# Layer 3 of a four-layer block: gate chain read by ScalarE, another lead-in, half of the partition copies issued on ScalarE's DMA queue

## The chip, the cores and the metric

The kernel runs on one core of a Trainium2 chip. The metric is the device time of one execution in microseconds (us). Before the change three runs gave 3566.73, 3568.6 and 3573.8 us; the median is 3568.6 us.

## The reference, cut to what matters

The input x has 4 samples of 256 channels on a 48 by 48 grid, in float32. Four layers follow each other, each of the form x + f(gn(x)), where gn is a group normalisation with 32 groups of 8 channels. Layers 0 to 2 are an attention with 8 heads, a gated depthwise filter, and an attention with one head that ends in a batch normalisation over all samples. Layer 3 is the one that the change is about:

```python
def _L3_conv_ref(x, attn_w1, attn_w2, refine_w, refine_b):
    p = jnp.mean(xw, axis=(2, 3))
    h = jax.nn.leaky_relu(p @ attn_w1.T, SLOPE)
    a = jax.nn.sigmoid(h @ attn_w2.T)
    y = xw * a[:, :, None, None]
    y = jax.lax.conv_general_dilated(y, refine_w, window_strides=(1, 1), padding='SAME', feature_group_count=C, ...)
    y = y + refine_b[None, :, None, None]
    mu = jnp.mean(y, axis=(2, 3), keepdims=True)
    var = jnp.mean(jnp.square(y - mu), axis=(2, 3), keepdims=True)
    y = (y - mu) * jax.lax.rsqrt(var + EPS)
    return jax.nn.leaky_relu(y, SLOPE)
...
x = x + _L2_conv_ref(_gn(x), ...)
x = x + _L3_conv_ref(_gn(x), ...)
```

So layer 3 is a 3 by 3 depthwise convolution of the normalised input, times a gate per channel and sample, then an instance normalisation, a leaky relu and the residual.

## The kernel before, in words

Channels lie on the 128 partitions, in two halves k = 0, 1. Layers 0 to 2 run first, with TensorE busy almost without a break in the attention of layer 2. The end of layer 2 and layer 3 are written out as one order per engine: within a `manual_schedule` scope every engine executes its instructions in the order in which the code emits them, and waits for others through semaphores.

**Layer 2's end.** The last attention unit is folded and divided (`fold`, `divide`, L389 to L395) on VectorE, `note` (L406 to L412) takes two sums of its denominators, `w_stats` (L1084) multiplies the last third of y by the output weights and takes `bn_stats`, and L1410 to L1433 turn these into the batch normalisation's scale `sc2` and offset `bi2` and into the means of the new x.

**Layer 3's tiles.** There are 8 tiles i, one for each sample and channel half (`TILES`). A tile's input is made by `w_product` (TensorE: output weights times y) and `grow` (VectorE, L1463: scale, add x, write into the padded image `pads`), with `border` (GpSimd) around it. The convolution is done on TensorE as 32 by 32 blocks: `shifted` holds, for each group of 32 channels j, copies of its padded image on the partitions of three of four groups q (`SHIFT`), and `products` (L1604) runs 12 matrix multiplications of this on 384 columns. The copies are made by `place` and `spread_out` (L1496 to L1511): for each half h of the rows, eight copies between different partition groups by DMA on SyncE's queue (SP), and four within a group, by GpSimd for h = 0 and on SP's DMA queue for h = 1. Each is 32 partitions by 1298 elements, 162.2 KB. Three `shifted` buffers take turns.

**Slots.** A tile i has six slots from t = 6 i, one for each sixth of its columns. `events` (L1747) holds for each slot a list of (rank, function), and the functions of a slot are emitted by rank: FRONT, CONV, PRODUCT, GROW, EVICT, SMALL, MOMENTS, SQUARE, SCALE, LAST, PLACE, STORE. For tile i, counted from its t:

- slots 0 to 5: `products` (CONV); slots 2, 4, 6: `evict` (ScalarE, L1616, two slots' PSUM to SBUF with a sum); slots 3, 5, 7: `square` of the result (ScalarE, L1627); slot 3: `centre` (VectorE)
- slot 8: `moments`, `scales` (VectorE, eight small instructions and GpSimd's power), `shift` under LAST
- slots 9, 10, 11: `scale` (ScalarE, L1681); slots 10, 11, 12: `leak` and `gain` (VectorE, L1687 and L1692, under LAST); slots 11, 12, 13: `store`
- slots -9, -8, -7: `w_product` and `grow` for the tile's three thirds; slots -8, -7, -6: squares of its input (ScalarE, L1487); slots -6 and -3: `spread_out` for h = 0, 1

The gate of a sample needs its group variance and two tiny layers. `Chain` (L1513) does this once per sample, so in even tiles: `total` (VectorE) and `groups` (TensorE) in slot 1, `inverse` (VectorE reads PSUM, GpSimd's power) in slot 2, `pooled` (VectorE) and `first_layer` (TensorE) in slot 3, `hidden` (VectorE reads PSUM) and `second_layer` (TensorE) in slot 4, `gate` (ScalarE reads PSUM) and `scaled` (VectorE) in slot 5. The chain's results in PSUM lie in unused columns of the convolution's own PSUM tile (`cv`), which holds two slots; three such tiles take turns. Its first member of a slot is emitted at FRONT, its second at SMALL:

```python
def put_chain(t, parts):
    for dt, (head, tail) in enumerate(parts):
        at(t + dt, FRONT, lambda fn=head: fn(None))
        if tail:
            at(t + dt, SMALL, lambda fn=tail: fn(now["ps"]))
```

The lead-in (L1405 to L1743) makes tiles 0 and 1 ahead of slot 0. Its copies for tile 0 go in part through ScalarE's DMA queue (`spread_out(0, h, nc.scalar)`, four per half).

Of the kernel before, what the change touches and what calls it, by code (L numbers as in the profile page):

```python
# [78 lines left out]
def usual_path(  # L79
# [333 lines left out]

    due, fills = {}, {}

# [13 lines left out]
    def last(u, t):  # L429

        take(u)
        if u.get("soon"):
            todo = [
                (fills, 1, lambda: total_here(u)), (due, 2, lambda: fold(u, nc.vector)),
                (due, 2, lambda: divide(u, nc.vector)), (due, 2, lambda: note(u)),
            ]
            after = 3
        else:
            todo = [
                (fills, AT_TOTAL, lambda: total(u)), (due, AT_FOLD, lambda: fold(u, nc.gpsimd)),  # L440
                (due, AT_INVERT, lambda: invert(u)),
                (due, AT_DIVIDE, lambda: divide(u, nc.gpsimd)),
            ]
            after = AT_AFTER
        todo += [(fills, after, fn) for fn in u["after"]]
        for when, dt, fn in todo:
            when.setdefault(t + dt, []).append(fn)
# [623 lines left out]

    def w_mul(b, k, c):

        ab = [pj_tile()[:, :SL] for _ in range(2)]
        for i, cc in enumerate(HALVES):
            for r, out in zip(HALVES, ab):
                c0 = k * P + i * D
                nc.tensor.matmul(
                    out[cc], lhsT=Ww[r, c0 : c0 + D],
                    rhs=y_of(b)[r, c * SL : (c + 1) * SL], start=True, stop=True,  # L1080
                )
        return [(c, ab[0]), (c + L2C, ab[1])]

    def w_stats(b, k, c):  # L1084
        for s, ps in w_mul(b, k, c):
            nc.vector.bn_stats(bst[:, k, b * NSL + s, :], ps)

    def l2_unit(b, c, s2):
        return {
            "pt": {}, "qc": slice(c * SL, (c + 1) * SL), "of": s2, "after": [],  # L1090
            "paired": PAIRED if b == B - 1 else range(NG), "scale": D ** -0.5,
            "soon": b == B - 1,
            "o": lambda: y_of(b)[:, c * SL : (c + 1) * SL],
        }
# [200 lines left out]
    for b in range(B):  # L1295
# [21 lines left out]
        else:  # L1317
            spread(work, stats(b, 0), [16, 17])
            spread(work, stats(b, 1), [23, 24])
            others.append((tap_matrices(), 1 + len(SHIFT), 4, 22))  # L1320
        phases.append(([l2_unit(b, c, twos[b]) for c in range(L2C)], work, others))
# [16 lines left out]
    attend(phases)  # L1338
    for b in range(NX):
        sample_means(b)  # L1340
    for k in range(NK):
        w_stats(B - 1, k, L2C - 1)
    strict.close()
# [60 lines left out]

    for sh in shifted:  # L1405
        nc.gpsimd.memset(sh[0:32, 2:4, :], 0.0)
    first = [w_product(0, c, cv_tile()) for c in range(L2C)]
    ahead = [w_product(1, 0, w_tile())]

    mv2 = lp.tile([P, NK, 2], F32, name="mv2")  # L1410
    for k in range(NK):
        nc.vector.bn_aggr(mv2[:, k, :], bst[:, k].rearrange("p s f -> p (s f)"))
    sc2 = lp.tile([P, NK], F32, name="sc2")
    var2 = lp.tile([P, NK], F32, name="var2")
    nc.vector.tensor_scalar(var2, mv2[:, :, 1], BN_EPS, None, ALU.add)
    rsqrt(sc2, var2)
    bi2 = lp.tile([P, NK], F32, name="bi2")
    nc.vector.tensor_add(bi2, mv2[:, :, 0], vec[:, V_WB, :])
    nc.vector.tensor_sub(bi2, vec[:, V_WB, :], bi2)
    sample_means(B - 1)  # L1420
    nc.vector.tensor_mul(sc2, sc2, vec[:, V_G2, :])
# [15 lines left out]

    of_groups = columns_of(first[0], B * NK)
    nc.tensor.matmul(
# [16 lines left out]

    def grow(i, c, ps):

        n, k = TILES[i]
        xs = XT[SEQ[n]][:, k, :].rearrange("p (h r c) -> p h r c", h=2, c=HW)  # L1460
        to = inside(i, c)
        for h in range(2):
            nc.vector.scalar_tensor_tensor(  # L1463
                to[:, h], ps[:, h, :SL].rearrange("p (r c) -> p r c", c=HW),
                sc2[:, k : k + 1], xs[:, h, c * RS : (c + 1) * RS, :], ALU.mult, ALU.add,
            )
# [28 lines left out]

    def place(i, h, j, q, eng):  # L1496
        to = shifted[(2 * i + h) % 3][32 * q : 32 * q + 32, j, :CL]
        c0 = h * HB * W2 + SHIFT[j, q]
        fr = pads[i % 4][32 * j : 32 * j + 32, c0 : c0 + CL]
        if eng is nc.gpsimd:  # L1500
            eng.tensor_copy(to, fr)
        else:
            eng.dma_start(to, fr)

    def spread_out(i, h, own=None):

        for j, q in SHIFT:
            if q != j:
                place(i, h, j, q, nc.sync)
        for j in range(4):  # L1510
            place(i, h, j, j, own or (nc.sync if h else nc.gpsimd))  # L1511

    class Chain:  # L1513
# [5 lines left out]
        def steps(self):  # L1519
            of, b = {}, self.b  # L1520

            def total(_):
                of["sq"] = sq = small.tile([P, NK], F32, tag="gn_sq", name="gn_sq")
# [4 lines left out]

            def groups(ps):
                of["ps"] = ps[:, 0:NK]  # L1530
                nc.tensor.matmul(of["ps"], lhsT=gmat, rhs=of["sq"], start=True, stop=True)

            def inverse(_):
                gv = small.tile([P, NK], F32, tag="gn_gv", name="gn_gv")
                nc.vector.tensor_scalar(gv, of["ps"], GN_EPS, None, ALU.add)
                of["rs"] = small.tile([P, NK], F32, tag="gn_rs", name="gn_rs", bufs=6)
                rsqrt(of["rs"], gv)

            def pooled(_):
                of["pm"] = pm = small.tile([P, NK], F32, tag="pm", name="pm")  # L1540
                nc.vector.tensor_mul(pm, dev[:, b, :], of["rs"])

            def first_layer(ps):
                of["ps"] = ps[0:D, 0:1]
                for k in range(NK):
# [4 lines left out]

            def hidden(_):
                raw = small.tile([D, 1], F32, tag="hraw", name="hraw")
                nc.vector.tensor_copy(raw, of["ps"])
                of["hl"] = hl = small.tile([D, 1], F32, tag="hl", name="hl")
                nc.vector.scalar_tensor_tensor(hl, raw, SLOPE, raw, ALU.mult, ALU.max)

            def second_layer(ps):
                of["ps"] = ps[:, 0:NK]
                for k in range(NK):
                    nc.tensor.matmul(  # L1560
                        ps[:, k : k + 1], lhsT=w2[:, k * P : (k + 1) * P], rhs=of["hl"],
                        start=True, stop=True,
                    )

            def gate(_):
                of["ga"] = small.tile([P, NK], F32, tag="ga", name="ga")
                nc.scalar.activation(of["ga"], of["ps"], AF.Exp, scale=-1.0)

            def scaled(_):
                ga = of["ga"]  # L1570
# [6 lines left out]

            return [
                (total, groups), (inverse, None), (pooled, first_layer), (hidden, second_layer),
                (gate, scaled),  # L1580
            ]
# [122 lines left out]
    def judge():  # L1704

        of = {}

        def lows(_):
            ok = lp.tile([P, 2, LW], F32, name="ok")
# [4 lines left out]

        def count(ps):
            of["ps"] = ps[0:1, 0:1]
            nc.tensor.matmul(of["ps"], lhsT=of["okm"], rhs=ones[:, 0:1], start=True, stop=True)

        def compare(_):
            nc.vector.tensor_scalar(sound, of["ps"], P - 0.5, None, ALU.is_ge)  # L1720

        return [(lows, count), (compare, None)]

# [3 lines left out]

    grow(0, 0, first[0])
    edges()
    border(0)  # L1730
    for c in range(1, L2C):
        grow(0, c, first[c])
    for h in range(2):
        spread_out(0, h, nc.scalar)
    centres()
# [9 lines left out]

    FRONT, CONV, PRODUCT, GROW, EVICT, SMALL, MOMENTS, SQUARE, SCALE, LAST, PLACE, STORE = range(12)
    events = {}  # L1747
# [6 lines left out]
    def put_chain(t, parts):  # L1754
        for dt, (head, tail) in enumerate(parts):
            at(t + dt, FRONT, lambda fn=head: fn(None))
            if tail:
                at(t + dt, SMALL, lambda fn=tail: fn(now["ps"]))

# [13 lines left out]
    def put_tile(t, cv, final):  # L1773
# [11 lines left out]
        at(t + 8, FRONT, cv.scales)  # L1785
        at(t + 8, LAST, cv.shift)
        for g in range(NG3):
            at(t + 9 + g, SCALE, lambda g=g: cv.scale(g))
            at(t + 10 + g, LAST, lambda g=g: cv.leak(g))
            at(t + 10 + g, LAST, lambda g=g: cv.gain(g))  # L1790
            at(t + 11 + g, STORE, lambda g=g: cv.store(g))

    def reload(k):
        nc.sync.dma_start(XT[0][:, k, :], x_out[:, k, :])

    for i, cv in enumerate(convs):
        t = i * NSL
# [6 lines left out]
        if i % NK == 0:  # L1804
            put_chain(t + 1, chains[i // NK].steps())
        if i < NK:
            at(t + 14, STORE, lambda k=cv.k: reload(k))
    put_chain(8, judge())
    T = len(convs) * NSL
    for t in range(max(T, max(events) + 1)):  # L1810
# [859 lines left out]
```

## Time and profile before

| what | value |
|---|---|
| median of three runs | 3568.6 us |
| the profiled execution's own time | 3567.38 us |
| its span, first to last instruction | 3565.7 us |
| TensorE busy, share of the span | 3436.9 us, 96% |
| VectorE, ScalarE, GpSimd busy | 2554.7, 2345.1, 805.9 us |
| mean granted TensorE clock | 0.987 |
| first and last convolution matmul (L1604) of layer 3 | 3389.13, 3546.6 us |
| copies into `shifted` by DMA, SP queue and ScalarE queue | 156 and 8, 162.2 KB each |
| the same by GpSimd (L1501) | 28, median 1286 ns |

Times in the timeline are us from the start of the span. A row of the timeline has the start, the length, the engine, the line, the operation, the tile written and the tiles read, and in brackets how long the engine was idle before it and what released it. PE is TensorE, PEld its weight loads, DVE VectorE, ACT ScalarE, POOL GpSimd; SPq and ACTq are the two queues' instruction streams, where a row is the issue of a transfer and not the transfer.

### The profile page before, as it was taken

The page shows a single profiled execution, that of the slowest core. Times are in us where ns is not written, and L with a number is a line of the kernel's source. Part 1 is how long each engine was busy: PE and PEld are TensorE (multiplying, and loading weights), DVE is VectorE, ACT ScalarE, POOL GpSimd, SP SyncE. Part 2 cuts the span into 40 slices and gives each one's busy share as a digit, 9 for nine tenths or more (in the row PEclk, how much of TensorE's full clock was granted, in tenths as well). Part 3 has the DMA queues.
Part 4 walks back from the last instruction along what each step waited for, and adds up shares of the span by engine and source line. Part 5 has one row for each costly group of instructions (what it writes and reads, how often), then busy time and mean ns, then how long its engine had stood idle before and what let it go on. Part 6 is the DMA issues. An engine that isn't in the chain of part 4 may idle for free. (4 is left out here: it accounts for less than half of the span.)

```text
span 3565.7 us, 88371 instructions
## 1 busy us (share of the span) xinstructions
PE 3436.9 (96%) x37036; PEld 1729.2 (48%) x37036; DVE 2554.7 (72%) x3472; ACT 2345.1 (66%) x3814; POOL 805.9 (23%) x615
## 2 busy tenths in 40 slices
PE   7999999999999999999999999999999999899886
PEld 4554555554444444444444444444444445565422
DVE  3455555567788788787887886878878878665856
ACT  4666666665886796658867965589678755555354
POOL 2333333321111010101001010111000126665432
PEclk9999999999999999999999999999999999999988
DMA  2211111111111111221111111111111100000087
GB/s 89 53 26 22 22 26 25 22 26 22 22 26 22 26 22 26 57 44 22 26 21 26 22 26 21 26 21 26 22 22 21 23 7 6 6 7 6 9 236 200
DMA packets 123575, 122.92 MB, mean 34 GB/s; under 512 B 59440, under 2 KB 113312, under 8 KB 122400
## 3 DMA queue, kind: packets, MB, share of 16 engines
q1 hardware_dynamic: 119456, 113.66, 16.6%
q8 instruction: 292, 4.78, 0.6%
q10 hardware_dynamic: 3712, 3.53, 0.4%
q14 instruction: 115, 0.94, 0.1%
HBM read 56.99 MB, written 11.80 MB: 19 GB/s over the span
## 5 line engine op out<-in xcount | busy, mean ns | idle before, releaser
L298 ACT ACTIVATE pt<-sc 128x768 f32<-128x768 f32 x1944 | 1475.2, 811 | 731.1 <-PE sc L292 722.9
L338 DVE TENSOR_TENSOR acc<-acc,pt 128x768 f32<-128x768 f32 x1368 | 1364.6, 997 | 173.1 <-ACT pt L298 72.8
L312 PE MATMUL av<-pt,v 64*64 64x384 f32 x13824 | 1274.8, 484 | 0.0
L292 PE MATMUL sc<-q,k 64*64 64x384 f32 x13824 | 1270.1, 482 | 0.8 <-ACT pt L298 0.8
L292 PEld LDWEIGHTS sc<-q,k 64*64 64x64 f32 x13824 | 525.2, 133 | 590.2 <-issue 543.1
L312 PEld LDWEIGHTS av<-pt,v 64*64 64x64 f32 x13824 | 518.1, 133 | 598.9 <-issue 565.9
L393 POOL TENSOR_TENSOR o<-o,rinv 128x384 f32<-128x384 f32 x95 | 120.8, 1271 | 1739.1 <-DMA rinv<-rinv 1730.0
L323 POOL TENSOR_TENSOR half<-pt 128x768 f32<-128x768 f32 x189 | 364.3, 1931 | 535.5 <-ACT pt L298 489.9
L338 DVE TENSOR_TENSOR acc<-acc,half 128x768 f32<-128x768 f32 x171 | 192.4, 1125 | 235.8 <-POOL half L323 234.8
L672 DVE SCALAR_TENSOR_TENSOR x<-pj,bo,x 128x384 f32<-128x384 f32 x192 | 118.4, 617 | 309.5 <-PE pj L659 308.2
L848 ACT ACTIVATE prod<-pd,wt 128x256 f32<-128x256 f32 x486 | 337.2, 765 | 0.2
L576 PE MATMUL pj<-xs,w 128*128 128x384 f32 (+1 forms) x720 | 275.4, 505 | 0.0
L576 PEld LDWEIGHTS pj<-xs,w 128*128 128x128 f32 x720 | 124.1, 189 | 127.9 <-issue 38.9
L312 PE MATMUL av<-pt,qv 64*64 64x384 f32 x1728 | 176.5, 497 | 0.0
L292 PE MATMUL sc<-qv,kd 64*64 64x384 f32 x1728 | 171.7, 487 | 2.4 <-ACT pt L298 2.4
L871 DVE TENSOR_REDUCE prod<-prod 128x256 f32<-128x1280 f32 x114 | 168.7, 1480 | 0.3 <-ACT prod L848 0.3
L659 PE MATMUL pj<-o,wo 128*128 128x384 f32 (+1 forms) x384 | 159.8, 499 | 5.7 <-issue 3.6
L607 PEld LDWEIGHTS pj<-w,xs 128*128 128x128 f32 x1080 | 134.5, 191 | 24.1 <-issue 1.2
L332 DVE TENSOR_TENSOR acc<-pt 128x768 f32<-128x768 f32 x99 | 119.9, 1212 | 26.6 <-ACT pt L298 26.6
L607 PE MATMUL pj<-w,xs 128*128 128x128 f32 x1080 | 134.9, 275 | 0.0
L389 POOL TENSOR_TENSOR o<-raw 128x384 f32<-128x384 f32 x95 | 121.0, 1273 | 44.6 <-ACT raw L385 44.6
L1604 PE MATMUL cv<-sh,taps 96*32 96x384 f32 (+1 forms) x1152 | 111.9, 524 | 10.0 <-DMA sh<-pad 8.6
(236 smaller groups left out, 2342.1 us busy)
## 6 DMA issues: line engine op xcount, KB each, us to landing
xs<-in_x_dram SPq DMA_DIRECT2D x90, 384.0 KB
sh<-pad SPq DMA_DIRECT2D x156, 162.2 KB
rinv<-rinv SPq DMA_DIRECT2D x208, 94.5 KB
out_dram<-x SPq DMA_DIRECT2D x24, 384.0 KB
l<-row SPq DMA_DIRECT2D x416, 1.5 KB
w<-in_wqkv_dram SPq DMA_DIRECT2D x32, 192.0 KB
x<-in_x_dram SPq DMA_DIRECT2D x4, 1152.0 KB
x<-in_x_dram SPq DMA_DIRECT2D x9, 384.0 KB
```

The lines of the kernel that those rows point to most:

```text
L292: nc.tensor.matmul(ps[c * D : (c + 1) * D, h, :SL], lhsT=u["of"]["k"][r, j0 : j0 + D], rhs=u["of"]["q"][r, u["qc"]], start=True, stop=True,)
L298: nc.scalar.activation(pt, ps[:, :, :SL], AF.Exp, scale=u["scale"])
L312: nc.tensor.matmul(u["av"][h * D : (h + 1) * D, half, :SL], lhsT=value(u, j, h)[r], rhs=pt[r, h, :], start=j == 0, stop=j == JB - 1,)
L323: nc.gpsimd.tensor_add(half, pts[0], pts[1])
L338: nc.vector.tensor_add(u["acc"], u["acc"], term)
L389: eng.tensor_add(u["sum"], u["raw"][:, 0, :], u["raw"][:, 1, :])
L393: eng.tensor_mul(o, o, u["rinv"])
L576: nc.tensor.matmul(ps[:, :n], lhsT=at["w"][:, k, t, :], rhs=xs[s][:, k, :n], start=k == 0, stop=k == NK - 1,)
L607: nc.tensor.matmul(ps[:, i * P : (i + 1) * P], lhsT=xs[s][:, k, i * P : (i + 1) * P], rhs=at["w"][:, k, 2, :], start=k == 0, stop=k == NK - 1,
L659: nc.tensor.matmul(ps[:, :n], lhsT=wo[:, p, k * P : (k + 1) * P], rhs=o["o"][:, :n], start=True, stop=True,)
L848: nc.scalar.activation(bufs[n % 3][:, :, min(n, 1) + i].rearrange("p (r c) -> p r c", c=AS), pd[:, PAD + dr : PAD + dr + AS, PAD + dc : PA ...
L871: nc.vector.tensor_reduce(to, bufs[n % 3][:, :, : min(n, 1) + len(taps)], AX.X, ALU.add)
```

## The change

1. **Layer 2's end.** The last two output products of layer 2 (`w_mul(..., wide=True)`) go to the score tiles of PSUM, so that both halves run without waiting for each other. Means of the first three samples and their common mean and variance (`sample_means`, `earlier`) move into the last attention phase; the last sample's are merged with a few small VectorE instructions. `note` of the last unit moves behind these.
2. **Lead-in.** The group matmul writes beside `first[2]` instead of `first[0]`; `grow` of tile 0 is done for the upper half of the rows first; only one `shifted` buffer is cleared ahead of it. The copies of tile 0 are spread (`spread_first`): 6 + 8 on SP's DMA queue, 1 on VectorE, 5 on ScalarE, 4 on GpSimd.
3. **Copies of tiles 1 to 7.** `spread_out` issues the eight copies per half in another order (`AWAY`), those from j < 2 on SP's queue and those from j >= 2 on ScalarE's; of the four in place for h = 1, two go to SP's queue and two are ScalarE copies.
4. **Gate chain.** It starts one slot later, its PSUM results are read by ScalarE (`read`), and two new ranks END and AFTER, behind all others, hold part of it. The vote on layer 2's denominators (`judge`) is read by ScalarE too.
5. **Last but one tile** (`soon`): its three `scale` go in one slot, and the last `leak`, `gain` and `store` one slot earlier.

```diff
+    def earlier(k):
+        n = (B - 1) * NSL
+        nc.vector.bn_aggr(mv3[:, k, :], bst[:, k, :n].rearrange("p s f -> p (s f)"))
...
+            spread(work, [lambda n=n: sample_means(n) for n in range(NX)], [7, 10, 15])
+            spread(work, [lambda k=k: earlier(k) for k in range(NK)], [18, 21])
...
-    for b in range(NX):
-        sample_means(b)
+    last_y = [w_mul(B - 1, k, L2C - 1, wide=True) for k in range(NK)]
     for k in range(NK):
-        w_stats(B - 1, k, L2C - 1)
+        for s, ps in last_y[k]:
+            nc.vector.bn_stats(bst[:, k, (B - 1) * NSL + s, :], ps)
+    sample_means(B - 1)
...
+    rsqrt(sc2, var2)
...
+    noted[0]()
...
-    for sh in shifted:
-        nc.gpsimd.memset(sh[0:32, 2:4, :], 0.0)
+    nc.gpsimd.memset(shifted[0][0:32, 2:4, :], 0.0)
...
+        if how == "sp":
+            nc.sync.dma_start(to, fr)
+        elif how == "actq":
+            nc.scalar.dma_start(to, fr)
+        elif how == "act":
+            nc.scalar.copy(to, fr)
...
+    AWAY = [(0, 1), (2, 3), (0, 2), (2, 1), (1, 0), (3, 2), (1, 2), (3, 1)]
+
+    def spread_out(i, h):
+        for j, q in AWAY:
+            place(i, h, j, q, "sp" if j < 2 else "actq")
         for j in range(4):
-            place(i, h, j, j, own or (nc.sync if h else nc.gpsimd))
+            place(i, h, j, j, ("sp", "act")[j % 2] if h else "pool")
+
+    def spread_first(h):
+        if h == 0:
+            how = dict(zip(AWAY, ("sp", "sp", "sp", "sp", "sp", "sp", "dve", "pool")))
+            how |= {(0, 0): "act", (1, 1): "act", (2, 2): "act", (3, 3): "pool"}
+        else:
+            how = dict.fromkeys(AWAY, "sp")
+            how |= {(0, 0): "act", (1, 1): "pool", (2, 2): "act", (3, 3): "pool"}
...
+            def read(p):
+                of["raw"] = small.tile([P, NK], F32, tag="chain", name="chain")
+                n = 1 if p < P else NK
+                nc.scalar.copy(of["raw"][0:p, 0:n], of["ps"])
...
             return [
-                (total, groups), (inverse, None), (pooled, first_layer), (hidden, second_layer),
-                (gate, scaled),
+                (0, FRONT, total), (0, SMALL, groups),
+                (1, FRONT, lambda: read(P)), (1, END, inverse),
+                (2, END, pooled), (2, AFTER, first_layer),
+                (3, AFTER, lambda: read(D)), (4, FRONT, hidden), (4, SMALL, second_layer),
+                (5, FRONT, gate), (5, END, scaled),
             ]
...
-    grow(0, 0, first[0])
+    for c in range(L2C - 1):
+        grow(0, c, first[c], [0])
     edges()
     border(0)
+    grow(0, L2C - 1, first[L2C - 1], [0])
+    grow(0, 0, first[0], [1])
+    spread_first(0)
+    for sh in shifted[1:]:
+        nc.gpsimd.memset(sh[0:32, 2:4, :], 0.0)
     for c in range(1, L2C):
-        grow(0, c, first[c])
-    for h in range(2):
-        spread_out(0, h, nc.scalar)
+        grow(0, c, first[c], [1])
+    spread_first(1)
...
-    FRONT, CONV, PRODUCT, GROW, EVICT, SMALL, MOMENTS, SQUARE, SCALE, LAST, PLACE, STORE = range(12)
+    FRONT, CONV, PRODUCT, GROW, EVICT, SMALL, MOMENTS, SQUARE = range(8)
+    SCALE, LAST, PLACE, STORE, END, AFTER = range(8, 14)
...
+        soon = t + 2 * NSL == T
         for g in range(NG3):
-            at(t + 9 + g, SCALE, lambda g=g: cv.scale(g))
-            at(t + 10 + g, LAST, lambda g=g: cv.leak(g))
-            at(t + 10 + g, LAST, lambda g=g: cv.gain(g))
-            at(t + 11 + g, STORE, lambda g=g: cv.store(g))
+            at(t + 9 + (0 if soon else g), SCALE, lambda g=g: cv.scale(g))
+            dt = 10 + (min(g, 1) if soon else g)
+            at(t + dt, LAST, lambda g=g: cv.leak(g))
+            at(t + dt, LAST, lambda g=g: cv.gain(g))
+            at(t + dt + 1 - soon, STORE, lambda g=g: cv.store(g))
...
-            put_chain(t + 1, chains[i // NK].steps())
+            put_chain(t + 2, chains[i // NK].steps())
```

## The prediction

> **What bounds the kernel now.** I read the page's busy shares and clock first, then a table by stage of layer 3, then TensorE's waits there, then the timeline round one of these waits.
>
> ```profile
> PE   7999999999999999999999999999999999899886
> ...
> PEclk9999999999999999999999999999999999999988
> DMA  2211111111111111221111111111111100000087
> ```
>
> TensorE fills every slice but the last two or three; these are layer 3, where the DMA engines are nearly full too. All that the change touches but a few instructions lies in the last 205 us. Convolution tiles 0 and 1, 2 and 3, 4 and 5, 6 and 7 are these four stages:
>
> ```profile
> 3398.00:3431.17 33.17, 31.31 (x343) 11.71 (x335) 14.27 (x38) 18.16 (x38) 7.42 (x10) 0.98 0.93 229
> 3431.17:3472.65 41.48, 33.58 (x351) 11.68 (x347) 30.13 (x57) 22.43 (x44) 15.41 (x15) 0.92 0.84 235
> 3472.65:3513.64 40.99, 33.42 (x350) 11.70 (x346) 29.49 (x56) 20.70 (x40) 15.40 (x15) 0.92 0.89 243
> ```
>
> Columns: stretch, its length, busy PE, PEld, DVE, ACT, POOL, clock, DMA share, GB/s. No engine is full in the 41 us of a pair: TensorE idles 8 us and loses clock, VectorE idles 11, ScalarE 19. So engines working in order wait for each other, and TensorE's waits (total, times, longest) say where:
>
> ```profile
> PE cv L1531 <- DVE gn_sq L1525: 15.2, 3, 5.1
> PE w L1398 <- DVE pad L1463: 4.5, 2, 2.4
> ...
> PE cv L1604 <- ACT ga L1567: 1.3, 4, 0.4
> PE cv L1604 <- DMA sh<-pad: 0.2, 1, 0.2
> ```
>
> The big one is the chain's `groups`, behind VectorE. The copies, 0.2 us, don't bound this stretch. The timeline of one such place:
>
> ```profile
> 3431.17 4.08 PE L1604 MATMUL cv<-sh,taps 96*32 96x384 f32 x48
> ...
> 3432.14 7.08 POOL L1501 COPY sh<-pad 32x1298 f32<-32x1298 f32 x4 [9.89 <-issue]
> ...
> 3438.11 1.90 DVE L1692 SCALAR_TENSOR_TENSOR x<-pad,bi,x 128x768 f32<-128x768 f32 x1
> 3439.94 0.15 DVE L1524 TENSOR_REDUCE gn_sq<-ssq 128x2 f32<-128x6 f32 x1
> ...
> 3440.33 0.59 PE L1531 MATMUL cv<-gn_sq,gmat 128*128 128x2 f32 x2 [5.09 <-DVE gn_sq L1525]
> 3440.85 5.42 PE L1604 MATMUL cv<-sh,taps 96*32 96x384 f32 x48
> ```
>
> Two slots of convolution take 4.08 us. Meanwhile VectorE does two leak and gain pairs, at 1.75 to 2.01 us an instruction beside GpSimd's copies (0.94 and 1.02 without), then `total`. TensorE waits 5.09 us and comes back slow: 5.42 us for the same 48 matmuls (6.90 and 6.84 in the next two pairs). Last, the lead-in:
>
> ```profile
> 3383.73 13.06 SPq L1503 DMA_DIRECT2D sh<-pad  x12
> 3383.77 9.10 ACTq L1503 DMA_DIRECT2D sh<-pad  x8
> ...
> 3389.13 1.46 PE L1604 MATMUL cv<-sh,taps 96*32 96x384 f32 x2 [4.48 <-DMA sh<-pad]
> ...
> 3392.92 0.94 ACT L1487 ACTIVATE junk<-pad,minus 128x768 bf16<-128x768 f32 x1 [27.45 <-DMA sh<-pad]
> ```
>
> Eight issues hold ScalarE's stream for 9.10 us, 1.14 each (0.51 to 1.79), and its next instruction runs only then. The first two slots of convolution, starved by copies, end at 3402.27.
>
> **What the Trainium skill says.** "DMA: Bandwidth & Descriptors", Issuing engines are not separate DMA queues: transfers from any engine run on the same 16 DMA engines; a second issuer saves only issue time. Agreed: 166 to 252 GB/s while both queues issued (one microsecond of 367), 229 to 243 with one. "SBUF — State Buffer", Who interferes with whom: a VectorE instruction with two SBUF inputs contends with a GpSimd instruction that reads SBUF. Agreed: 0.95 against 2.0 us. "TensorE: Matmul & The Clock Gate", What's actually happening: after an idle window of about 3.4 us the clock halves. The trace agrees after 5 us, but 2.39 us of idling also cost 1.64 us of slow matmuls once, and 2.16 us nothing. "PSUM — Partial Sum Buffer", Engine vs sequencer instructions: ScalarE and VectorE queues are strict FIFO, as in the trace.
>
> **The change part by part.** The sum stands on the profiled 3567.38 us (span 3565.7 plus 1.7 around it); the median is 1.2 us above.
>
> *Layer 2's end.* Products without a wait for `bst` save 0.8 us; `note`'s four VectorE instructions (3370.61 to 3371.82, 1.2 us) now lie between the power and its first use and give 0.8 back. The moved aggregates, 3 x 2 x 0.25 + 2 x 0.75 = 3 us of VectorE, lie under full TensorE in the last attention phase, where VectorE idles over 25% (22.50 of 30 us busy); uncovered they cost up to 3. Net 0.
>
> *Lead-in.* Only four `grow` halves precede the upper copies, against six, and no wait of 0.70 for the group matmul: copies start near 3382.5, 1.2 earlier. Upper copies on DMA are 6, not 12: 1 MB at 240 to 280 GB/s is 4 us, plus 1.3 from issue to first data (3383.73 to 3385) and about 0.7 to land: slot 0 starts at 3388.5. ScalarE's three copies (384 elements 0.49 us, 768 elements 0.80, so 1298 some 1.23 each; "ScalarE: Activation LUTs", What ACT_TABLE_LOAD costs, gives 0.19 + 0.83 ns an element, 1.27) and GpSimd's two (1.3 to 1.9) end before that. Two slots at slow clock take 5.4 to 6.9: 3395; slot 2 to 3397. Then `groups`, and ScalarE's `read`, after five copies (6.2), six squares (6.3) and four queue issues (2.4, less what overlaps), near 3398. Slot 3 starts at 3398.3, against 3402.58 + 2.04 = 3404.6. **-6.3** (-4 to -8).
>
> *ScalarE's load.* Per tile now 3 evictions, 6 squares, 3 scales: 12.0 us. Added: 8 issues, 2 copies (2.5). An issue costs 0.51 (shortest) to 1.14 (lead-in mean); I take 0.6, SP's median being 0.589, half of it beneath the instruction before: 2.4. So 17 us, at worst 12.0 + 2.5 + 9.1 = 23.6. Behind each four issues wait, in slot 0 of a tile, the square that `moments` needs and in odd tiles `gate`; in slot 3, two copies, then eviction, square and the scale that `leak` needs. SP's queue loses ten issues per tile and isn't waited for. Fourteen fewer 162 KB copies in tiles 1 to 7 (9 us of DMA) shorten nothing while TensorE waits 0.2 us for DMA.
>
> *Chain, `groups`.* `total` now comes in slot 2, behind `moments` and `scales` (3440.20 to 3441.65, 1.5 us). From the end of tile 1's last product, VectorE needs `grow` 1.1, two contended pairs 7.5, these 1.5, `total` 0.35: 10.7. TensorE has three slots, 6.1. Wait 4.7, plus 0.4 because the next slot writes the PSUM tile that `read` reads (`gate` holds TensorE in this way now, 0.26 to 0.42). Before: 5.1. **0 a pair.**
>
> *Chain, `pooled`.* At END of slot 4 it stands behind `grow`, `leak`, `gain` of that slot: product's end + 1.2 + 1.95 + 0.15; `first_layer` waits for it ahead of slot 5's convolution. **+3.3**, in tiles 2 and 4. In tile 0 there is no `leak` yet: 1.4. In tile 6 no product: 0.
>
> *Chain, `hidden`.* In the next tile's slot 0 it stands behind slot 5's `grow` 1.2 and contended pair 3.9; TensorE has one slot, 2.04, then `second_layer` waits. **+3.3** (0 after tile 0; about 1 after tile 6, whose pair is not contended).
>
> *What goes.* The 2.39 and 2.16 us waits for `pad` in tiles 3 and 5: with `scaled` out of slot 5 VectorE is ready (product + 11 us) before slot 3's product. **-2.3**. Clock: two more waits above 3 us and one less of 2.3: 0 to +3, I take +1.6. Per middle pair: 3.3 + 3.3 + 0.4 - 2.3 - 0.1 + 1.6 = **+6.2**.
>
> *First and last pair.* First: +1.4, and `gate` behind `evict`, a square and four issues +2.5, less the waits that go (2.0): +1.9. Last: +0.4, +1 and slow clock 1: +2.4. `soon` puts a pair (1.95) ahead of the last statistics and takes it from the end: 0.
>
> Sum: -6.3 + 1.9 + 2 x 6.2 + 2.4 = +10.4: 3577.8; I say 3578.
>
> **The rivals.**
> - *ScalarE becomes the bound.* For: each issue held it 1.14 us when both queues were loaded, and DMA is 84 to 93% busy. Against: 0.589 is usual. Then a tile takes 23.6 us and a pair some 47 plus 4 of ScalarE's own waits: +10 a pair over two and a half pairs: 3567.4 - 4.4 + 25 = 3588; I say 3590. Chance 0.18.
> - *The new waits are covered.* `first_layer` and `hidden` meet slack I don't see, as TensorE is held up already by `groups`; pairs stay at 41 us: 3567.4 - 6.3 + 1.9 = 3563. Against: each wait is counted from the product just before it. Chance 0.20.
> - *Faster.* VectorE's pairs no longer meet GpSimd's copies, as ScalarE's evictions and scales, free of VectorE, come earlier. Uncontended, `total` is ready 1.1 + 3.9 + 1.5 + 0.35 = 6.9 us after the product, a wait of 0.8, with no clock loss; the mechanism decides from leak and gain below about 1.3 us each. A pair then gains 5, the last too: 3563 - 15 = 3548. Against: both start with the same `grow`, and the change leaves GpSimd's h = 0 copies in place. Chance 0.12.
>
> **How the numbers follow.** My forecast, chance 0.50, has its own range from 3570 to 3587. 0.2% is 7 us, about what a measurement of this kernel can tell from no change, so "same" is 3561.5 to 3575.7. A quarter of the forecast is below 3575.7. Slower: 0.37 + 0.18 = 0.55. Same: 0.13 + 0.11 = 0.24. Faster: 0.09 + 0.12 = 0.21. The range is 3557 to 3594: it leaves out most of the fast rival and the tail of the first one.
>
> **What would show it.** Right: first two convolution slots end near 3395; TensorE waits of over 3 us at `first_layer` and `second_layer` on VectorE, `groups` still near 4.7; middle pairs of 45 to 48 us. Wrong: pairs of 41 us or less, `leak` near 0.95 us in slot 0; or ScalarE without idle time and queue issues above 1 us, which is the first rival.

## The result and the profile after

The changed kernel takes 3591.1 us (median of 5, 3585.5 to 3595.1) against 3567.4 for the kernel before on the same chip (5 runs, 3566.7 to 3573.8): a ratio of 1.006, 95% interval 1.0048 to 1.0072. It is slower by 0.6%. Its profiled execution took 3586.3 us with a span of 3584.5, so 18.9 more than the profile of before (3567.4 and 3565.7). It is the second fastest of the five, so the stages below account for these 18.9 us and not for the 23.7 between the medians. The first product of layer 2's last y starts anywhere between 3367 and 3375 us in the profiles shown here, whatever the kernel. So stages are compared by their lengths, and a few us between two medians are no finding by themselves.

Two rows of the page of the changed kernel:

```profile
PEclk9999999999999999999999999999999999999888
DMA  2211111111111111211111111111111100000275
```

The slow-down is in the last three slices: the granted clock now falls in three slices, not two, and the DMA engines, nearly full before (8, 7), are not (2, 7, 5). The table by stage has the lead-in, the rest of tiles 0 and 1, the tile pairs 2-3 and 4-5, and tiles 6 and 7 (columns as in the prediction):

```profile
3369.78:3405.43 35.65, 25.06 (x168) 10.78 (x170) 14.94 (x44) 17.07 (x24) 19.75 (x18) 0.71 0.54 128
3405.43:3432.50 27.07, 23.57 (x251) 7.75 (x250) 12.05 (x33) 15.44 (x30) 6.82 (x8) 0.94 0.58 140
3432.50:3482.66 50.16, 37.80 (x350) 14.54 (x347) 29.64 (x57) 26.96 (x50) 16.72 (x15) 0.83 0.77 213
3482.66:3533.61 50.95, 38.64 (x350) 14.53 (x346) 29.59 (x56) 28.91 (x51) 16.71 (x15) 0.83 0.62 166
3533.61:3565.85 32.24, 27.00 (x302) 12.88 (x298) 22.54 (x49) 19.49 (x34) 8.68 (x7) 0.95 0.58 168
```

The two middle pairs are 8.7 and 10.0 us longer (41.48 and 40.99 before). VectorE does the same 29.6 us of work, ScalarE 27 to 29 where it did 21 to 22, and the clock is 0.83 where it was 0.92. TensorE's waits from the end of the lead-in on (total, times, longest):

```profile
PE cv L1587 <- DVE gn_sq L1581: 13.9, 3, 4.7
PE cv L1615 <- DVE hl L1610: 7.9, 2, 3.9
PE cv L1602 <- DVE pm L1597: 7.8, 3, 3.3
PE cv L1662 <- ACT ga L1622: 2.9, 4, 2.1
```

`groups` waits about as before (4.7 us against 5.1). `second_layer` (L1615, for `hidden`) and `first_layer` (L1602, for `pooled`) wait anew, in each middle pair 3.93 and 3.26 us. From these waits alone the chain's new places seem to explain everything. The timeline of tile 2's slots 3 to 5 shows a second delay, which no wait of TensorE names:

```profile
3443.84 0.33 SPq L1862 DMA_DIRECT2D x<-x_out  x1
...
3445.01 8.55 ACTq L1535 DMA_DIRECT2D sh<-pad  x2
...
3453.60 2.57 ACT L1537 COPY sh<-pad 32x1298 f32<-32x1298 f32 x2 [7.80 <-DMA sh<-pad]
...
3455.56 0.56 PE L1602 MATMUL cv<-pm,w 128*64 128x1 f32 x4 [3.26 <-DVE pm L1597]
...
3456.05 3.60 PE L1662 MATMUL cv<-sh,taps 96*32 96x384 f32 x24
```

ScalarE stands still for 7.80 us, with an issue to its queue pending, and TensorE's wait at the end of that time is put down to VectorE. What the issue waits for stands in the trace's records of issues, with the semaphore that each copy counts up when it lands (time, queue, which of the shared semaphores it waits for and gives; a reload, L1862, brings half of the first sample's x back from `x_out`):

```
3443.84 SP   reload        gives 106
3444.26 SP   copy, tile 3  gives 107
3445.01 ACT  copy, tile 3  waits 105, gives 105
3451.52 SP   copy, tile 3  waits 106, gives 106
3453.04 ACT  copy, tile 3  waits 107, gives 107
```

In these records all copies, stores and reloads of both queues use eight semaphores in turn (100 and 102 to 108). Each of the 166 issues from 3378 us on comes after the earlier transfer on its semaphore has landed. So ScalarE's fourth issue waits 6.92 us for a copy of SP's queue that was issued behind a reload of 1152 KB and landed at 3453.02. The kernel has two reloads, issued at 3443.84 and 3471.64, both in tiles 2 and 3; every other wait of an issue on ScalarE's queue is 2.1 us or shorter. In the lead-in the same coupling works the other way round:

```profile
3384.73 10.04 PE L1662 MATMUL cv<-sh,taps 96*32 96x384 f32 x72 [2.11 <-DMA sh<-pad]
...
3392.07 1.22 ACTq L1535 DMA_DIRECT2D sh<-pad  x2
...
3400.84 4.59 PE L1662 MATMUL cv<-sh,taps 96*32 96x384 f32 x22 [4.38 <-DMA sh<-pad]
```

Slots 0 to 2 end at 3394.8, 2 us ahead of the forecast's 3397, but slot 3 then waits for tile 0's lower copies: SP's fifth waited 7.3 us, until 3394.61, for semaphore 107, which tile 1's first copy on ScalarE's queue held. That one was issued at 3392.07, behind ScalarE's five copies and six squares.

### The profile page after: what moved, and what is told of

The parts are those of the page before. It is cut to its first block, busy times and chain, and to the rows that moved or that the text cites. A ratio compares the mean times of both kernels' runs of the same rounds, so it can differ in the third digit from the quotient of the medians.

```text
span 3584.5 us, 88368 instructions
## 1 busy us (share of the span) xinstructions
PE 3445.1 (96%) x37036; PEld 1738.4 (48%) x37036; DVE 2562.0 (71%) x3475; ACT 2369.4 (66%) x3842; POOL 815.6 (23%) x619
## 3 DMA queue, kind: packets, MB, share of 16 engines
q1 hardware_dynamic: 116000, 101.69, 15.4%
## 5 line engine op out<-in xcount | busy, mean ns | idle before, releaser
L389 POOL TENSOR_TENSOR o<-raw 128x384 f32<-128x384 f32 x95 | 123.7, 1302 | 41.9 <-ACT raw L385 41.8
L1662 PE MATMUL cv<-sh,taps 96*32 96x384 f32 (+1 forms) x1152 | 121.8, 559 | 10.7 <-DMA sh<-pad 6.5
```

The lines of the kernel that those rows point to most:

```text
L389: eng.tensor_add(u["sum"], u["raw"][:, 0, :], u["raw"][:, 1, :])
L1662: nc.tensor.matmul(out[32 * j : 32 * j + 32], lhsT=made["taps3"][held, self.k, dr, j, :], rhs=sh[held, j, r0 + dr : r0 + dr + RS, 0:HW], s ...
```

## The experiments

Two theories went in. **Placement**: TensorE waits because `pooled` and `hidden` stand behind leak and gain on VectorE. **Queue**: ScalarE's issues hold ScalarE, and TensorE behind it; its form for the lead-in is **coupling** through the shared semaphores. All times are medians; the ratio is to the kernel before in the same job (3567.0 to 3569.7 us). "Pairs" are the two distances from one `groups` to the next.

| run | queues for upper copies | chain | us | ratio, 95% | pairs, us |
|---|---|---|---|---|---|
| before | one | old | 3567 to 3570 | 1 | 41.4, 41.1 |
| after | two | changed | 3591.1 | 1.0048 to 1.0072 | 50.1, 51.0 |
| e1 | one | changed | 3576.8 | 1.0015 to 1.0033 | 50.1, 50.9 |
| e2 | two, old lead-in | old | 3587.5 | 1.0036 to 1.0063 | 46.8, 44.6 |
| e3 | two | old | 3584.0 | 1.0031 to 1.0058 | 46.6, 47.2 |
| e4 | two | early | 3588.3 | 1.0038 to 1.0065 | 54.8, 41.9 |
| e5 | one | early | 3558.2 | 0.9952 to 0.9975 | 39.4, 40.3 |
| e6 | one | old | 3563.8 | 0.9975 to 0.9991 | 42.9, 41.5 |
| e7 | one, idle load | early | 3572.1 | 0.9999 to 1.0016 | 43.8, 45.5 |
| e8 | two | laid out anew | 3570.9 | 1.0000 to 1.0017 | 47.9, 39.1 |
| e9 | one | laid out anew | 3548.3 | 0.9923 to 0.9950 | 36.7, 38.5 |
| e10 | one | anew, `groups` in slot 2 | 3555.2 | 0.9959 to 0.9980 | 42.5, 38.6 |
| e11 | one | anew, `groups` in slot 3 | 3548.3 | 0.9929 to 0.9956 | 43.9, 31.4 |
| e12 | two, tile 1's h=0 one | changed | 3582.3 | 1.0022 to 1.0043 | 49.6, 50.8 |

**e1, one queue.**

```diff
-            place(i, h, j, q, "sp" if j < 2 else "actq")
+            place(i, h, j, q, "sp")
```

> All eight upper copies of each half tile go back to SP's queue; everything else is as in the changed kernel (3586.3 us in the profiled run). Placement theory (TensorE waits because the chain's steps stand behind leak and gain on VectorE): the three waits at groups, first_layer and second_layer stay at 4.7, 3.3 and 3.9 us, middle pairs stay at 48 to 51 us. Queue theory (eight issues a tile hold ScalarE, and TensorE behind it): middle pairs fall to 43 us or less, -15 us or more in all. Coupling theory, for the lead-in only: in the changed kernel the compiled order makes the last four copies of tile 0's lower half on SP's queue wait for completion semaphores that tile 1's four copies on ScalarE's queue hold; with one queue that wait goes, slot 3 of tile 0 starts near 3397 instead of 3400.8 (-4 us), and the wait of 2.1 us for the gate in tile 1 goes too. Placement and coupling together: 3578 to 3582; queue: 3571 or less.

14 us below the changed kernel, and not in the pairs: the first three rows of TensorE's waits shown above stand in e1's answer word for word. The gain is in the lead-in (from the first product of layer 2's last y to slot 3 of tile 0: 25.0 us; 31.1 in the changed kernel; 33.9 before), in tile 1's gate, and in the slow matmuls behind both. Placement gets its waits and pairs, and coupling gets its earlier slot 3 and the end of the wait for tile 1's gate; the time is 1.2 us below the range of both together. The queue theory fails here.

**e2, the queue alone.** The kernel before, with the new order and places of the copies in tiles 1 to 7 only.

```diff
-        for j, q in SHIFT:
-            if q != j:
-                place(i, h, j, q, nc.sync)
...
+        for j, q in AWAY:
+            place(i, h, j, q, "sp" if j < 2 else "actq")
...
```

> The kernel before (3567.4 us) with the new spreading of copies alone: the new order, upper copies with j of 2 and 3 on ScalarE's queue and two lower own copies on ScalarE in tiles 1 to 7; tile 0's copies, the lead-in and the chain as before. Placement theory: middle pairs stay at 41 to 42 us, the time within 4 us of before. Queue theory: ScalarE's load of some 17 us or more a tile shows in TensorE's waits, middle pairs of 45 to 50 us, +10 to +20 us.

20 us above before (13 to 22 by the interval), against placement's forecast of 4. With the chain of before, whose steps come early, TensorE waits 12.5 us in four pieces (longest 5.0) for `gate` on ScalarE. No issue on ScalarE's queue waits more than 1.7 us here, so this loss is not one long standing still. The new order and the two ScalarE copies are in e6 too, whose pairs are 42.9 and 41.5. So the queue costs about as much as the whole change, on a kernel without the other cause.

**e3, the chain of before** in the changed kernel (its `steps`, `judge`, `put_chain` at t + 1).

> The changed kernel with the chain of before (its steps, its slots, VectorE reading PSUM, one slot earlier); lead-in, copies and the queue stay changed. Placement theory: the waits at first_layer and second_layer go, groups stays near 5 us, middle pairs return to 41 to 43 us, so -16 to -18 us against the changed kernel: 3568 to 3571. Queue theory: middle pairs stay near 50 us and the time near 3586.

7 us below the changed kernel by the medians, where placement wanted 16 to 18; the two intervals overlap, and from the first product of layer 2's last y to the end the profiles have 214.8 and 214.7 us. The waits at `first_layer` and `second_layer` went, the middle pairs are some 4 us shorter each, and 11.4 us of waits for `gate` on ScalarE came. Neither theory had this: taking the VectorE delay away uncovers ScalarE's.

**e4, two steps early.**

```diff
-                (2, END, pooled), (2, AFTER, first_layer),
-                (3, AFTER, lambda: read(D)), (4, FRONT, hidden), (4, SMALL, second_layer),
+                (2, FRONT, pooled), (2, AFTER, first_layer),
+                (3, FRONT, lambda: read(D)), (3, MOMENTS, hidden), (4, SMALL, second_layer),
```

> The changed kernel with two of the chain's steps moved and nothing else: pooled to the front of its slot 4, hidden into slot 5 behind grow and ahead of leak and gain (its read on ScalarE to the front of slot 5). Placement theory: the waits of 3.3 and 3.9 us at first_layer and second_layer fall below 0.6 us, the slow matmuls behind them go with them (some 2 us), groups keeps its 4.7 us; middle pairs of 41 to 43 us, -16 to -20 us in all: 3566 to 3570. Queue theory, or a VectorE that is simply late wherever the step stands: the waits only move to the next reader and the middle pairs stay above 47 us.

Nothing gained in all (3588). The timeline of its tile 2 says why:

```profile
3449.06 8.58 ACTq L1535 DMA_DIRECT2D sh<-pad  x2
...
3455.34 0.39 PE L1602 MATMUL cv<-pm,w 128*64 128x1 f32 x4
...
3457.68 2.57 ACT L1537 COPY sh<-pad 32x1298 f32<-32x1298 f32 x2 [7.83 <-DMA sh<-pad]
...
3463.05 0.14 ACT L1575 COPY chain<-cv 64x1 f32<-64x1 f32 x1
...
3463.24 4.07 PE L1662 MATMUL cv<-sh,taps 96*32 96x384 f32 x24 [7.50 <-ACT chain L1575]
```

`first_layer` no longer waits, but the next slot needs `read` on ScalarE, which is stuck for 7.83 us and then has a queue of work; TensorE waits 7.50. ScalarE's two long waits of an issue, 6.9 and 5.8 us, each follow one of the two reloads. Tiles 4 and 5, where no reload is issued, show the opposite. There are the two `groups` round them:

```profile
3502.12 0.59 PE L1587 MATMUL cv<-gn_sq,gmat 128*128 128x2 f32 x2 [6.28 <-DVE gn_sq L1581]
...
3543.98 0.59 PE L1587 MATMUL cv<-gn_sq,gmat 128*128 128x2 f32 x2 [5.06 <-DVE gn_sq L1581]
```

This pair takes 41.9 us where the changed kernel takes 51.0 with the same two queues: here the early steps alone gain 9 us. Placement gets its number in one pair and the queue theory in the other.

**e5, e4's steps and one queue**, both edits together.

> Both edits that were tried alone, together: one queue for the upper copies (alone 3577) and pooled and hidden ahead of leak and gain (alone 3588, no gain). Two-causes theory: in the changed kernel two delays of about equal length lie side by side in each pair of tiles, ScalarE stuck behind issues on its queue (7 to 8 us in one piece) and the chain behind VectorE's leak and gain (3.3 + 3.9 us), and each hides the other; only taking both away gains. Then the waits at first_layer, second_layer, gate and read are all below 0.6 us, groups keeps 4.7, middle pairs of 41 to 43 us, 3556 to 3562. Placement-is-harmless theory (VectorE is late wherever the steps stand, the queue was the only cause): middle pairs stay near 50 us and the time at 3574 to 3579.

3558.2, as the two-causes theory said: 33 us below the changed kernel, where the edits alone gave 14 and 3 (from layer 2's last y to the end of the profiles 32, 12 and 1). But the theory does not hold in each pair, as it was put. In tiles 2 and 3 only both edits together gain: 50.1 us with one queue, 54.8 with early steps, 39.4 with both, and there two delays do lie side by side. In tiles 4 and 5 the early steps alone reach 41.9, and the one queue adds 1.6. Of TensorE's waits after the lead-in these are left:

```profile
PE cv L1587 <- DVE gn_sq L1581: 14.3, 3, 5.0
PE w L1442 <- DVE pad L1495: 2.5, 2, 1.4
PE cv L1662 <- ACT chain L1575: 1.7, 7, 0.2
PE cv L1662 <- ACT ga L1622: 1.0, 4, 0.3
```

**e6, one queue and the chain of before.**

> One queue and the chain of before, with the changed lead-in: what is left of the change is its lead-in, the order of the copies, two lower own copies on ScalarE and the last pair. Two-causes theory: middle pairs return to 41 to 42 us, the lead-in keeps the 9 us that the one-queue run showed, 3556 to 3562. If the chain of before was costly by itself beside the new lead-in: above 3570.

3563.8, just above the range given, but on that side: what is left of the change, its lead-in above all, gains 0.1 to 0.25%.

**e7, issuing without its waits.** e5, and at each place of an issue a copy on ScalarE that nobody reads.

```diff
+            if j > 1:
+                busy = lp.tile([P, 512], F32, tag="busy", name="busy", bufs=2)
+                nc.scalar.copy(busy, idle)
```

> As the run with one queue and early steps, plus eight copies of 128x512 elements per tile on ScalarE (about 0.6 us each, writing a tile that nobody reads) at the places where the changed kernel issues its eight copies: ScalarE's load of issuing without its waits. Coupling theory (ScalarE stands still because an issue waits for a completion semaphore that the other queue's copies, stores and reload hold): within 4 us of the run without these copies, no wait of 7 us on ScalarE. Issue-load theory: 10 us or more above that run, with waits for gate and read of 2 to 7 us as in the changed kernel with early steps alone.

The copies took 0.612 us each, the issues 0.604 (median). 14 us above e5: the issue-load theory gets its number and the coupling theory misses its own. The waits fit coupling better: `gate` waits at most 2.0 us, `read` at most 1.8, and ScalarE has no standing still of 7 us. The three stretches between one `groups` and the next say more than the total. The idle copies make them 4.4, 4.4 and 5.2 us longer than in e5; the real issues (e4 against e5) 12.4, 15.4 and 1.6. So plain load costs about the same everywhere, while the queue's price lies in the lead-in and the first tiles, and beside the reloads. In the third stretch the idle copies cost more than the real issues: they are an upper bound for load, since an issue can lie partly beneath the instruction before it. One wait of 7.57 us at `groups`, put down to a copy, stays unexplained.

**e12, tile 1's first four copies back on SP's queue.**

```diff
-            place(i, h, j, q, "sp" if j < 2 else "actq")
+            place(i, h, j, q, "sp" if j < 2 or i == 1 and h == 0 else "actq")
```

> The changed kernel with only the four copies of tile 1's upper half (h = 0) moved from ScalarE's queue to SP's. Coupling theory of the lead-in: tile 0's last four copies then wait for no semaphore of ScalarE's queue, so slot 3 of tile 0 starts about 26 us after layer 2's last y instead of 31.1; by the compiled order tile 1's second copy on SP's queue now waits for ScalarE's first issue in slot 3, so up to 3 us can come back as a wait for copies at tile 1's first slot. Middle pairs stay at 50 to 51 us: 2 to 6 us below the changed kernel, 3581 to 3588. Issue-load theory of the lead-in: slot 3 gains at most the 2.4 us of four issues.

TensorE at slot 3 of tile 0 and at slot 3 of tile 1:

```profile
3399.08 2.45 PE L1662 MATMUL cv<-sh,taps 96*32 96x384 f32 x24 [0.25 <-ACT chain L1575]
...
3419.71 2.13 PE L1662 MATMUL cv<-sh,taps 128*32 128x384 f32 x20 [0.78 <-DMA sh<-pad]
```

Slot 3 starts 25.7 us after layer 2's last y (3373.34), 5.3 earlier than in the changed kernel, with no wait for copies; four issues' load, 2.4, can't give that, and e7, with that load and one queue, has 27.5 (e5, without the load, 25.7). Of the 3 us allowed, 0.78 came back, at slot 3 of tile 1 and not at its first slot. So it is the coupling that took most of the lead-in's gain. The pairs stay at 50 us, though in this profile no issue on ScalarE's queue waits more than 2.1 us: the chain's places are enough for that.

**e9, the chain laid out anew, one queue.**

```diff
+                (0, SQUARE + 0.5, total), (1, SMALL, groups),
+                (2, FRONT, lambda: read(P)), (2, END, inverse),
+                (3, FRONT, pooled), (3, SMALL, first_layer),
+                (4, FRONT, lambda: read(D)), (4, MOMENTS, hidden), (5, SMALL, second_layer),
+                (6, FRONT, gate), (6, MOMENTS, scaled),
...
-            put_chain(t + 2, chains[i // NK].steps())
+            put_chain(t, chains[i // NK].steps())
```

> One queue, and the whole chain laid out anew: total in slot 0 ahead of that slot's leak and gain, groups in slot 1, inverse in 2, pooled and first_layer in 3, hidden in 4 ahead of leak and gain, second_layer in 5, gate and scaled in slot 0 of the next tile. Two-causes theory: the wait of 4.7 us at groups goes as well, and the slow matmuls behind it (some 2.3 us): middle pairs of 35 to 38 us, 3543 to 3550, faster than both kernels. If VectorE's 29.6 us of work in a pair bound the pair through buffers or other waits: the wait moves to pad or scales, pairs near 41, 3556 to 3562.

3548.3 us, 0.5 to 0.8% below before, with pairs of

```profile
3425.80:3462.51 36.71, 30.93 (x346) 11.82 (x347) 28.23 (x56) 27.53 (x48) 17.38 (x16) 0.99 0.86 243
3462.51:3501.01 38.50, 33.33 (x346) 11.84 (x346) 27.86 (x56) 27.64 (x50) 15.40 (x15) 0.92 1.00 269
```

The second fills the DMA engines. `groups` still waits 3.42 us, as `total` waits for the last square on ScalarE.

**e8, the same chain with two queues.**

> The chain laid out anew as in the run at 3548, but with the changed kernel's two queues. The second queue cost 30 us with the early steps (3588 against 3558: 14 of issue load, which the run with idle copies showed, 16 of standing still). If that price belongs to the queue and not to one layout of the chain: 3575 to 3582, with waits of TensorE for read or gate on ScalarE. If the new layout leaves ScalarE more slack: below 3562.

3570.9, between both forecasts: the queue costs 23 us in this layout too, though TensorE's waits are now for VectorE (`groups` up to 7.1 us), whose `total` waits for ScalarE's last square (2.59 us there). ScalarE waits 19.7 us in all, 6.6 at most, for copies. Its two long waits of an issue, 5.3 and 5.4 us, are for the semaphores of the two reloads; in tiles 4 and 5 the pair takes 39.1 us, 0.6 more than in e9.

**e10 and e11, `groups` one and two slots later than in e9.**

> As the run at 3548 (one queue, chain laid out anew), with groups and every later step of the chain one slot later; total stays where it is. In that run total waits for the last square on ScalarE, and groups still waits 3.42 us in the middle pairs, followed by slow matmuls. A slot is 2.04 us: if total's time is fixed by ScalarE, the wait falls to 1.4 us or less and its slow matmuls (up to 2.8 us) go: 3 to 8 us off, 3540 to 3545. If the copies bound the pair by now (DMA share 0.86 and 1.00 in the two middle pairs): TensorE waits for copies in their place, within 2 us of 3548.

> As the run at 3548 with groups in slot 3 instead of 1, and the later steps two slots later (first_layer 5, second_layer in slot 1 of the next tile, gate and scaled at the front of its slot 2). The run with groups in slot 2 was slower, 3555, because read on ScalarE then held TensorE for 1.1 to 4.9 us: slots 2 and 3 share one PSUM tile, and the next slot can't write it before ScalarE, behind other work, has read. Parity theory: in the odd slots 1, 3, 5 the next slot has another PSUM tile, so no read holds TensorE; groups waits under 0.5 us; 3538 to 3545. If ScalarE's lateness reaches TensorE anyway, through scaled in front of scales: pairs above 38 us, above 3550.

e10 missed: `groups` waits 0.2 to 1.5 us, but 7 us were lost. From its timeline:

```profile
3435.88 4.07 PE L1662 MATMUL cv<-sh,taps 96*32 96x384 f32 x24 [4.86 <-ACT chain L1575]
```

Slots 2g and 2g + 1 share a PSUM tile, so after a chain step in an even slot the next slot waits until ScalarE has read. In e11, in odd slots, no `read` holds TensorE, as expected, and one pair took 31.4 us; but it ends level with e9, above the 3538 to 3545 expected, since copies (5.25 us once) and `pooled` (6.23) wait instead. 3548 is the best of all, by two ways.

## Why the prediction was right or wrong

The direction, and the place of most of the loss, were right; the profile rose by 18.9 where the sum said 10.4. The median, 3591.1, lies above the forecast's own range, 3570 to 3587, and next to the first rival's 3590. Both are luck: the wide range reached so far up to make room for that rival, and the rival's signs, ScalarE without idle time and issues above 1 us, didn't come (ScalarE busy 27 of 50 us in the first middle pair, an issue 0.60 at the median). The difference, by stages (forecast in brackets): layer 2 -1.0 (0), lead-in to the start of slot 3 -2.8 (-6.3), from there to tile 2 +5.1 (+1.9), middle pairs +8.7 and +10.0 (+6.2 each), last pair -1.2 (+2.4).

- **Lead-in: the failed step.** "Slot 3 starts at 3398.3" counted ScalarE's and GpSimd's work and the copies' volume, not that SP's copies could wait for ScalarE's queue. Slots 0 to 2 did end by 3395. e12 and e1 show what the step would have been worth: -8.1 and -8.9. The trace of before already had the sign. The 9.10 us read as eight issues of 1.14 are 6.85 us of issues, 0.86 each, and 2.26 between them, nearly all of it before the last three, which wait for semaphores; and a copy on SP's queue, issued at 3395.33, starts 0.02 us after a copy of ScalarE's queue landed on the semaphore that it waits for.
- **First pair.** `gate` behind four issues: 2.07 us against the 2.5 taken. `pooled` in tile 0: 1.33 against 1.4. The rest is slot 3, starved and slow: 4.59 us for 22 matmuls.
- **`groups`, `pooled`, `hidden`:** 4.6 to 4.7, 3.26 and 3.93 us against 4.7, 3.3 and 3.3; the waits for `pad` after tile 1 went, as said. `hidden` came out longer because it takes 1.21 us itself beside GpSimd's copies.
- **Clock: the mis-sized term.** Taken +1.6 a pair. In the first middle pair 24 matmuls took 4.42 us after `groups` and 3.60 after `pooled` (2.14 at full clock) and 72 took 8.45 after `hidden` (6.01): 6.2 us in all, where before it was 1.3 and 1.6. That is +3.2 for +1.6, and with `hidden`'s extra 0.6 accounts for 2.2 of the 2.5 missing there. In the second pair the same places and one product cost 7.4 us where it was 2.8 before: +4.5, outside the 0 to +3 that was allowed, and with `hidden` 3.5 of the 3.8 missing. (The pair's sum also has +0.4 and -0.1 beside a `groups` already set at 0; that is 0.3 us.)
- **Last pair.** Neither `hidden`'s wait nor the extra slow clock came: 48 matmuls after `groups` took 5.68 us where they took 6.84 before, and `groups` itself 4.61 where it waited 5.09.
- **ScalarE's load, and the first rival.** The issue's price, 0.6, was right, and ScalarE did not become full. But it was wrong to give the queue no price of its own beyond that load: alone it costs 20 us on the kernel before (e2). The rival saw load only; e7 puts load at up to 14 us, without ScalarE's long waits.

So the forecast's mechanism is real (e1: with one queue it still makes pairs of 50 us; e5 removes it and gains 19 more). In tiles 4 and 5 it is the cause: taken away alone, it gives back 9 us (e4). In tiles 2 and 3 it isn't the cause by itself: ScalarE's wait behind a reload, of similar length, lies beside it, and in the lead-in the coupling took most of the gain. Each alone costs much of the whole: the queue 20 us (e2 against before), the chain 13 (e1 against e6). The rival with covered waits fails, and so does "faster": leak and gain still took 1.74 to 2.01 us beside GpSimd's copies. "PSUM — Partial Sum Buffer", Engine vs sequencer instructions, gives the rule that makes a stuck issue costly: ScalarE's queue is strict FIFO. The trace agrees: two copies of the same padded image that the issue at 3445.01 reads stood for 7.80 us behind the next issue. The second issuer, of which the prediction quotes that it saves only issue time, saved none here that TensorE waited for, and cost 14 to 30 us (e1, e2, e8, e4).

Open: how much of the loss goes with the shared semaphores. In the records of all six runs with two queues, every issue on ScalarE's queue in layer 3 that stood over 0.3 us starts within 0.03 us of a landing on the semaphore that it waits for. But e2 loses 20 us with short waits only, and neither a kernel with two queues and separate semaphores nor one with the reloads elsewhere was run.

## What to carry to other kernels

A DMA issued from a compute engine is an instruction that can wait: look up which semaphore it reuses and which transfer holds it before moving copies there. When undoing a suspected cause gains nothing, look at each stage by itself (e4 lost 5 us in one pair and gained 9 in the next), and try it together with the next cause before dropping it; a wait names only the delay that ended last. In an ordered pipeline put a small dependent step ahead of long work on its engine, and into a slot whose PSUM tile the next slot doesn't write.

## What the runs showed of the hardware

A short pause of TensorE can cost clock, and its length alone doesn't say whether it will. After 2.07 us of idling (`gate`, tile 1) 72 matmuls took 7.43 us against 6.01. Two pauses of 1.79 us in e7 were followed by 72 in 6.01 and in 7.71 us, one of 2.41 us in e4 by 72 in 6.01. "TensorE: Matmul & The Clock Gate", What's actually happening, has an idle window of about 3.4 us that runs freely. All these pauses are shorter, so the runs show more than the page says: 2 us can't be taken as free.

An issue to ScalarE's queue for a copy of 32x1298 elements held it for 0.51 to 1.43 us in the changed kernel, median 0.60, as long as a ScalarE copy of 512 elements for each partition (0.61). That is without the wait for its semaphore, which came to 6.92 us once.
